# GEGLU of the second layer 5.7 batches behind its cross attention instead of 9, with x kept on chip between them

## The chip, the cores and the metric

The kernel runs on one core of one Trainium2 chip. The core has a TensorE (PE in the profile, with its weight loads listed apart as PEld), a VectorE (DVE), a ScalarE (ACT), a GpSimd (POOL), and a SyncE (SP), whose queue issues nearly all transfers of this kernel. The metric is device time in microseconds; lower is better. Each time is a median of several runs of the whole program. The profile is one separate execution of it.

## The reference

A tensor x of 32 batches of 112 rows and 256 columns goes through four layers that share one context of 32 times 375 rows and 256 columns. All is float32. Cut to what matters here:

```python
x = L0(x, ctx)        # grouped cross attention
# layer 1: three sublayers, each with a layernorm, a residual, and fake quantisation in the two attentions
x = attn(ln1(x), ln1(x), ...) + x                 # self attention       "l1s"
x = attn(ln2(x), context, ...) + x                # cross attention      "l1x"
hg = ln3(x) @ ff_w1 + ff_b1                       # GEGLU                "l1f"
a, g = split(hg, 2)
x = a * gelu(g, approximate=False) @ ff_w2 + ff_b2 + x
x = L2(x, ctx, ctx)   # cross attention "l2x" and feed-forward "l2f"
x = L3(ctx, x)        # causal self attention "l3s", cross attention "l3x", feed-forward "l3f"
```

`ff_w1` has 256 rows and 2048 columns, `ff_w2` 1024 rows and 256 columns. One batch does not depend on another, and a batch passes the sublayers in order.

## The kernel before

A **sweep** is one sublayer taken over all 32 batches. There are nine: `l0x, l1s, l1x, l1f, l2x, l2f, l3s, l3x, l3f`. A sweep is a list of **units** (one batch, or a pair of batches, `GB = 2`), and a unit is a list of **slots**: 8 per batch in `l1x` (two heads each), 4 per batch in `l1s` (four heads each), 8 per pair of batches in `l1f` (128 hidden columns each). A slot has stages (scores, softmax, transpose, product with V, closing step). `LAGS` says how many slots of its own sweep later each further stage is issued. Work that prepares a unit (loading x, layernorm statistics, applying the norm, projections) is a list of **atoms**, and `LEAD` says how many slots ahead of its place each atom is issued.

Sweeps run in pairs (`PAIRS`): `l0x` with `l1s`, `l1x` with `l1f`, `l2x` alone, `l2f` with `l3s`, `l3x` with `l3f`. `order` gives every slot a place on a planner's axis, in planner's units. A pair takes `dur` units per batch, the sum of its `SPAN` values (14 + 8 = 22 for `l1x` and `l1f`), and its second sweep starts `off` units after the first:

```python
off = max(GB * dur + self.DELAY[s] * dur, done + self.GAP - t0) if q else 0.0
```

`done` is where the pair ahead ends. For `l1f` the first term is 2 x 22 + 5 x 22 = 154. The pair ahead (`l0x` and `l1s`) ends 170 units after `l1x` has begun, so the second is 170 + 30 = 200, and `l1f` runs 200 units, or 9.1 batches, behind `l1x`. The ends overlap: `l1s` is still at work for the first 170 units of `l1x`, and `l1f` is alone for the last 200, since `l2x` begins where it ends (`OVER`).

**How x travels.** Within the pairs `l0x`/`l1s` and `l3x`/`l3f` the second sweep takes over the tile that the first one has written (`beside`). `l1x` and `l1f` are named in `AGAIN`: each loads x once for its norm and once more, late (the atom `again`), for its residual, and `l1x` stores its x to memory. All x tiles are of tag `x` with 11 buffers. During `l1x` the loads and stores of x are held back (`later`) and issued behind the next transposing transfer of `l1x` (`behind`), of which there are four per batch.

**Small tiles** have tags with buffers of their own: `ki` (6) for the quantised keys and the float tiles ahead of them, `ot` (7) for quantised queries, attention outputs and the split hidden tiles of `l2f` and `l3f`, `pp2` (4) for the softmax of four heads in `l1s` and `l3s` and for the masked queries of `l1x` (`queries_apart`).

The Python code issues instructions in the order of this plan. A scheduler that knows the buffers then settles each engine's instruction order and writes the semaphores. Each engine runs its list strictly in order. Lines that the text speaks of: L1126 scores of `l1x` (and of `l3x`), L1179 scores of `l1s` (and `l3s`), L1254 and L1294 the two products of `l1f`, L1283 its gate times value on VectorE, L458 the transposes of a normalised x, L456 the normalising itself, L441 the norm's statistics, L1227 the residual of `l1x`, L847 that of `l1f`, L386 the load of x, L411 its store, L900 the masked queries, L788 the scores of `l2x`.

Of the kernel before, what the change touches and what calls it, by code (L numbers as in the profile page):

```python
# [8 lines left out]
F32 = mybir.dt.float32  # L9
# [8 lines left out]
S = 112  # L18
# [42 lines left out]

class Kern:

    BUFS = dict(w=8, x=11, xh=4, ki=6, s1=9, sm=32, ot=7, pp2=4, k3=11, h=3, qs=2, k6=5)
    PBUFS = dict(sc=3, ps1=4, acc=1)

    LAGS = dict(
# [11 lines left out]
    LEAD = dict(  # L79
        l0x=dict(load=11, stats=10, apply=6, cload=11, cstats=8, cut=8, ctrans=5, q=4, k=[2, -2], v=-1),  # L80
        l1s=dict(load=5, stats=5, apply=3, q=2, k=2, v=1),
        l1x=dict(load=17, stats=12, apply=10, cload=14, cut=14, q=8, apart=[2, -1], k=4, v=-1, v2=[-2, -4, -6, -7], again=-7),
        l1f=dict(load=13, stats=11, apply=10, gate=2, gelu=1, again=-3),
        l2x=dict(load=10, stats=7, apply=6, cload=11, cut=7, q=4, k=[1, 1], v=0, vload=2),
        l2f=dict(load=6, stats=5, apply=3),
        l3s=dict(load=10, stats=8, apply=7, q=7, qload=3, k=6, v=3, c2=4, k2=1, v2=1),
# [285 lines left out]

    def beside(self, i):

        return any(self.sweeps[i : i + 2] == list(p) for p in PAIRS) and self.sweeps[i] not in self.AGAIN


    AGAIN = ("l1x", "l1f")

    def load_x(self, s, b):  # L380
        i = self.sweeps.index(s)
# [250 lines left out]
    def softmax4(self, sc, scale=None):  # L632

        nc = self.nc
        p = self.t([S, 4, S], F32, "pp2")
        sm = self.t([S, 4], F32, "sm")
        nm = self.t([S, 4], F32, "sm")
        nc.vector.tensor_reduce(nm, sc, AX.X, ALU.max, negate=True)
        if self.turn("exp4") == 1:
            nc.vector.tensor_tensor(p, sc, nm.unsqueeze(2).to_broadcast([S, 4, S]), ALU.add)  # L640
            nc.scalar.activation(p, p, AF.Exp, scale=1.0 if scale is None else scale)
            nc.vector.tensor_reduce(sm, p, AX.X, ALU.add)
            return p, sm
# [98 lines left out]
    def unit64(self, s, b0, i, qd, gb, W, g, cx, wd, wq, wk, wv, gqa, gkv, gvec, bvec):  # L742
# [33 lines left out]
        def mk(m):  # L776
# [22 lines left out]
            def c():  # L799
                if m == 0:  # L800
                    return
                vq = kv["v"]
                av = self.ps([128, 2, S])
                for mm in range(1 if gqa else 2):
                    for a in range(3):
                        ta = slice(a * S, (a + 1) * S)
                        for j in range(2):
                            hd = qd if gqa else 2 * mm + j
                            o = av[64 * j : 64 * j + 64]
                            nc.tensor.matmul(  # L810
                                o if gqa else o[:, mm, :],
                                vq[:, a, hd * 64 : hd * 64 + 64],
                                st["pt"][:, :, j, ta] if gqa else st["pt", mm][:, j, ta],
                                start=a == 0,
                                stop=a == 2,
                            )
                ot = st["ot"] = self.t([128, 2, 2, S], F32R, "ot")
# [25 lines left out]

    def residual(self, s, b0, g):

        for e, x in enumerate(g["xr" if s in self.AGAIN else "x"]):
            self.nc.vector.tensor_tensor(x, g["acc"][:, e, :], x, ALU.add)  # L847
            self.store_x(s, b0 + e, x)

# [46 lines left out]

    def queries_apart(self, i, c, bs):

        t = self.t([128, 8, S], BF16, "pp2")
        self.nc.gpsimd.tensor_tensor(  # L900
            t,
            i[:, c, bs].unsqueeze(1).to_broadcast([128, 8, S]),
            self.own.unsqueeze(2).to_broadcast([128, 8, S]),
            ALU.mult,
        )
        return t

    def fkq(self, ps, inv, shape):

        nc = self.nc  # L910
        p = shape[0]
        f = self.t(shape, F32, "ki")
        self.scale("fk", f, ps, inv[:p], MAGIC)
        self.eng("clip").tensor_scalar(f, f, MAGIC + 127.0, MAGIC - 128.0, ALU.min, ALU.max)
        return f

    def qk_atoms(self, lead, w, src, W, isq, quant, prm, put, tag=None, keep=None, apart=False):
# [4 lines left out]
        def half(c):  # L922
            if quant and c == 0:
                both = isq and not apart
                z["i"] = self.t([128, 2, 2, W] if both else [128, 2, W], BF16, "ot" if isq else "ki")
# [94 lines left out]
    def unit16(self, s, b0, i, gb, g, wd, quant, self_attn, qb, kb, vb, dl, gvec, bvec):  # L1020
# [54 lines left out]
        def av(heads, pt, first, octets, ahead=True):  # L1075
# [21 lines left out]
                        )  # L1097
            if octets:
                if octets[0] == 0:
                    st["ot"] = self.t([128, 2, 2, S], F32R, "ot")  # L1100
                oc = slice(octets[0], octets[-1] + 1)
                hi, lo = st["ot"][:, 0, oc, :], st["ot"][:, 1, oc, :]
                o = o[:, : len(octets), :]
# [60 lines left out]
        def quad(qd):  # L1164
# [28 lines left out]
            def b():  # L1193
                if quant:
                    z["pt"] = pt = self.t([128, 4, S], BF16, "s1")
                    nc.sync.dma_start_transpose(pt, z["pq"].rearrange("p h t -> p (h t)"))
                    return
                pst = self.ps([128, 4, S])
                for j in range(4):
                    nc.tensor.transpose(pst[:S, j, :], z["p"][:, j, :], self.ident[:S, :S])  # L1200
                z["pt"] = self.t([S, 4, S], F32, "pp2")
                self.copy("copy", z["pt"], pst[:S])

            def c():
# [13 lines left out]
        u.slots = [quad(qd) for qd in range(4)] if self_attn else [pair(pr) for pr in range(8)]  # L1218

        def fin():  # L1220
            x = st["xr"] if s in self.AGAIN else g["x"][i]
            po = self.ps([S, D])
            wo = wd["o"]
            self.bias_mm(s, po)
# [3 lines left out]
            self.store_x(s, b0 + i, x)  # L1228

        u.slots[-1].st[4] = fin  # L1230
        if s in self.AGAIN:
            u.atoms.append((L["again"], 0, lambda: st.update(xr=self.load_x(s, b0 + i))))
        return u


# [3 lines left out]
    def unitff(self, s, b0, gb, wd, gvec, bvec, b1, glu):  # L1239
# [33 lines left out]
        def mk(c):  # L1273
            z = {}

            def a():
# [10 lines left out]
                ul = z["ul"] = self.t([128, 2, W], F32R, "ot")  # L1287
                self.split(uu, ul[:, 0, :], ul[:, 1, :], ("upper", "lower"))

            def b():  # L1290
# [15 lines left out]
            return Slot(a, None, b)  # L1306

        u.slots = [mk(c) for c in range(8)]
        if s in self.AGAIN:
            u.atoms.append((L["again"], 0, lambda: g.update(xr=[self.load_x(s, b0 + i) for i in range(gb)])))  # L1310
        return u


# [40 lines left out]
    def order(self, units):  # L1354
# [5 lines left out]
        for p in [p for p in pairs if p]:  # L1360
# [4 lines left out]
            last = len(p)  # L1365
            for q, s in enumerate(p):
                n = sum(len(u.slots) for u in units[s])
                off = max(GB * dur + self.DELAY[s] * dur, done + self.GAP - t0) if q else 0.0
                k = 0
                for ui, u in enumerate(units[s]):  # L1370
                    for sl in u.slots:
# [4 lines left out]
        ev.sort(key=lambda e: e[:4])  # L1376
        return [(e[4], e[2], e[5]) for e in ev]

    DELAY = dict(l1s=3, l1f=5, l3s=3, l3f=2)
    GAP = 30.0  # L1380
    PAUSE = 4
    OVER = dict(l2x=0.0, l3x=34.0)

    def run(self):
# [231 lines left out]
```

## Time and profile before

| | |
|---|---|
| median of 3 runs | 4890.22 us (4889.1 to 4894.96) |
| profiled execution: time, span | 4897.09 us, 4895.3 us |
| TensorE busy, weight loads | 4482.3 us (92%), 3983.4 us (81%) |
| VectorE, ScalarE, GpSimd busy | 74%, 70%, 43% |
| mean granted TensorE clock | 0.963 |
| DMA | 674.54 MB, mean 138 GB/s |

The profile's page gives the busy share of each engine, a row of 40 slices of the span, and the chain of work that ended last. Several sweeps follow each other, so the share over the whole span is a mean over stages. A view by windows gives the same for chosen stretches of time, together with the clock that TensorE was granted. The view of one source line shows when its instructions ran, and so where a sweep begins and ends: the first score of `l1x` is at 1150 us, the last score of `l1s` at 1428 us, the first product of `l1f` at 1459 us, the last score of `l1x` at 2249 us, the first score of `l2x` at 2349 us.

### The profile page before, as it was taken

What the parts mean: (1) busy time and instruction counts of PE and PEld (TensorE: products, weight loads), DVE (VectorE), ACT (ScalarE), POOL (GpSimd) and SP (SyncE); (2) the same over time, 40 slices, a digit from 0 to 9 for tenths busy, and PEclk for the clock granted to TensorE, in tenths of its full rate; (3) what the DMA queues carried; (4) which work ended last, traced back from release to release, by engine and by line L of the source; (5) the groups of instructions that cost most, each with busy time, mean ns of one, the idle gap of its engine ahead of it and who ended that gap; (6) DMA issues with size and microseconds to landing.
All of it is one profiled execution on the core that took longest, in us unless ns stands there. A gap on an engine that the chain in (4) does not pass through costs nothing.

```text
span 4895.3 us, 111536 instructions
## 1 busy us (share of the span) xinstructions
PE 4482.3 (92%) x37824; PEld 3983.4 (81%) x37824; DVE 3618.5 (74%) x9806; ACT 3406.4 (70%) x10644; POOL 2119.8 (43%) x3674
## 2 busy tenths in 40 slices
PE   6999999998778999999999999998999886898999
PEld 5888888886667888888999999997888885787878
DVE  4788888888888888885788888886555554777776
ACT  4788888887767777774677777774555444677776
POOL 4455555555443333432333333334333332566665
PEclk9999999999889999999999999999999997999999
DMA  4433333334666565664455555543666667666663
GB/s 103 126 85 86 82 85 86 84 78 123 139 132 137 140 150 146 151 161 119 129 142 144 142 144 143 143 130 112 197 188 184 200 182 205 169 168 163 162 162 85
DMA packets 585415, 674.54 MB, mean 138 GB/s; under 512 B 318688, under 2 KB 495056, under 8 KB 584656
## 3 DMA queue, kind: packets, MB, share of 16 engines
q1 hardware_dynamic: 584848, 667.40, 52.2%
q8 instruction: 305, 5.00, 0.5%
q14 instruction: 262, 2.15, 0.1%
HBM read 323.55 MB, written 173.02 MB: 101 GB/s over the span
## 4 chain that ended last, share of the span: by engine, by line
PE 39%; DMA 7%; DVE 5%; ACT 1%; issue 1%; SPq 1%; POOL 1%; ACTq 0%; DVEq 0%; POOLq 0%
PE ps L679 6%; PE ps L235 5%; PE ps L236 4%; PE ps L237 4%; PE sc L788 3%; PE ps L810 3%; PE ps L1090 3%; DMA qs<-dq_l3s 2%; PE sc L1126 2%; DMA k<-cd 2%; PE acc L235 1%; PE acc L237 1%; PE acc L236 1%; PE ps L1254 1%; DVE sm L621 1%
## 5 line engine op out<-in xcount | busy, mean ns | idle before, releaser
L217 POOL TENSOR_SCALAR k<-k,sm 112x375 f32<-112x375 f32 (+1 forms) x1536 | 936.7, 622 | 1036.0 <-DVE sm L661 459.6
L200 ACT ACTIVATE k<-ps 125x336 f32<-125x336 f32 (+4 forms) x2005 | 914.0, 469 | 425.4 <-PE ps L237 185.9
L621 DVE TENSOR_REDUCE sm<-sc 112x1 f32<-112x375 f32 x1792 | 944.8, 539 | 150.0 <-PE sc L788 89.7
L627 ACT ACTIVATE k<-sc,sm 112x375 f32<-112x375 f32 x1536 | 881.2, 579 | 104.1 <-DVE sm L621 84.7
L679 PE MATMUL ps<-ident,k 112*125 112x112 f32 x4608 | 733.2, 277 | 15.2 <-issue 4.0
L679 PEld LDWEIGHTS ps<-ident,k 112*125 112x125 f32 x4608 | 649.2, 190 | 71.7 <-issue 43.7
L788 PE MATMUL sc<-k,qs 128*112 128x376 f32 x2048 | 539.9, 356 | 19.9 <-ACT k L627 9.7
L235 PE MATMUL ps<-w,k 128*125 128x256 f32 (+2 forms) x1344 | 431.4, 321 | 30.6 <-ACT k L627 15.5
L235 PE MATMUL ps<-h,w 128*128 128x224 f32 x1408 | 410.9, 299 | 43.4 <-DVE h L202 17.1
L710 DVE TENSOR_TENSOR k<-ps,k 64x376 fp32r<-64x376 f32 x640 | 350.2, 547 | 123.3 <-ACT k L200 108.0
L202 DVE COPY k<-ps 125x336 f32<-125x336 f32 (+2 forms) x619 | 289.3, 468 | 170.3 <-PE ps L237 69.5
L236 PE MATMUL ps<-h,w 128*128 128x224 f32 x1408 | 393.7, 282 | 0.8 <-DVE h L231 0.5
L237 PE MATMUL ps<-h,w 128*128 128x224 f32 x1408 | 392.8, 282 | 0.0
L236 PE MATMUL ps<-w,k 128*125 128x256 f32 (+2 forms) x1344 | 390.6, 291 | 0.0
L237 PE MATMUL ps<-w,k 128*125 128x256 f32 (+2 forms) x1344 | 389.4, 290 | 0.0
L235 PE MATMUL ps<-k,w 128*128 128x376 f32 x896 | 341.3, 381 | 41.4 <-DMA k<-cd 26.1
L810 PE MATMUL ps<-k,k 125*64 125x112 f32 (+1 forms) x4608 | 350.0, 296 | 3.6 <-DVE k L202 1.5
L213 POOL TENSOR_SCALAR k<-k,sm 112x375 f32<-112x375 f32 x256 | 165.5, 647 | 416.5 <-DVE sm L661 326.6
L788 PEld LDWEIGHTS sc<-k,qs 128*112 128x112 f32 x2048 | 304.1, 177 | 49.3 <-ACT k L627 24.4
L235 PEld LDWEIGHTS ps<-w,k 128*125 128x125 f32 (+2 forms) x1344 | 264.0, 196 | 79.0 <-ACT k L627 26.7
L235 PEld LDWEIGHTS ps<-h,w 128*128 128x128 f32 x1408 | 273.2, 197 | 67.3 <-issue 29.7
L627 ACT ACTIVATION_READ_ACCUMULATOR k<-sc,sm 112x1 f32 x1536 | 324.0, 211 | 0.0
(213 smaller groups left out, 12592.3 us busy)
## 6 DMA issues: line engine op xcount, KB each, us to landing
qs<-h SPq DMA_DIRECT2D x512, 224.0 KB
k<-k SPq DMA_DIRECT2D x192, 376.0 KB
k<-cd SPq DMA_DIRECT2D x64, 752.0 KB
vd<-k SPq DMA_DIRECT2D x128, 375.0 KB
k<-vd SPq DMA_DIRECT2D x128, 375.0 KB
qs<-dq_l3s SPq DMA_DIRECT2D x256, 112.0 KB
qs<-dq_l3x SPq DMA_DIRECT2D x256, 112.0 KB
x<-xd SPq DMA_DIRECT2D x224, 112.0 KB
```

The costliest lines, as they stand in the source:

```text
L200: self.nc.scalar.activation(out, in_, AF.Identity)
L202: self.nc.vector.tensor_copy(out, in_)
L217: self.nc.gpsimd.tensor_scalar(out, in_, by, 1.0, ALU.mult, ALU.mult)
L235: mm(out, lhs(0), rhs(0), start=start, stop=False)
L236: mm(out, lhs(0), rhs(1), start=False, stop=False)
L237: mm(out, lhs(1), rhs(0), start=False, stop=stop)
L621: nc.vector.tensor_reduce(nms[j], sc[j][:, :n], AX.X, ALU.max, negate=True)
L627: nc.scalar.activation(p[:, j, :n], sc[j][:, :n], AF.Exp, bias=nms[j], scale=1.0 if scale is None else scale, accum_out=sm[:, j : j + 1])
L679: self.nc.tensor.transpose(pst[:TB, a * S : (a + 1) * S], p[:, j, a * TB : (a + 1) * TB], self.ident[:S, :S])
L710: nc.vector.tensor_tensor(ks[o, j, :], pk[r, :TE], ks[r, j, :].bitcast(F32), ALU.subtract)
L788: nc.tensor.matmul(sc[:, :TE], qs[:, hd, q, bs], kk, start=q == 0, stop=q == 1)
L810: nc.tensor.matmul(o if gqa else o[:, mm, :], vq[:, a, hd * 64 : hd * 64 + 64], st["pt"][:, :, j, ta] if gqa else st["pt", mm][:, j, ta], ...
```

## The change

`AGAIN` is taken out. `l1x` and `l1f` are now a pair like the others: `l1x` loads x once, adds its residual into the same tile, `l1f` takes its norm from that tile and adds its own residual into it, and stores it. That takes out 32 stores and 96 loads of x (112 x 256 float32 each). The tag `x` has 13 buffers instead of 11.

`DELAY` of `l1f` goes from 5 to 3 and `GAP` becomes a value per sweep, -44 for `l1f` (30 for `l3s` and `l3f` as before, 0 for `l1s`, for which the first term decides as before). `off` of `l1f` is then max(44 + 66, 170 - 44) = 126 units, or 5.7 batches. `l1f` starts 44 units before the end of `l1s`.

`ki`, `ot` and `pp2` become one tag, `m`, with 15 buffers (17 in the three before). The leads follow: `l1x` loads x 14 slots ahead instead of 17, `l1f` takes x, its statistics and its norm 10 slots ahead (13, 11 and 10 before). Past the last slot of `l1x`, its outstanding stages are issued at half the distance.

```diff
-    BUFS = dict(w=8, x=11, xh=4, ki=6, s1=9, sm=32, ot=7, pp2=4, k3=11, h=3, qs=2, k6=5)
+    BUFS = dict(w=8, x=13, xh=4, m=15, s1=9, sm=32, k3=11, h=3, qs=2, k6=5)
...
-        l1x=dict(load=17, stats=12, apply=10, cload=14, cut=14, q=8, apart=[2, -1], k=4, v=-1, v2=[-2, -4, -6, -7], again=-7),
-        l1f=dict(load=13, stats=11, apply=10, gate=2, gelu=1, again=-3),
+        l1x=dict(load=14, stats=12, apply=10, cload=14, cut=14, q=8, apart=[2, -1], k=4, v=-1, v2=[-2, -4, -6, -7]),
+        l1f=dict(load=10, stats=10, apply=10, gate=2, gelu=1),
...
     def beside(self, i):
 
-        return any(self.sweeps[i : i + 2] == list(p) for p in PAIRS) and self.sweeps[i] not in self.AGAIN
-
-
-    AGAIN = ("l1x", "l1f")
+        return any(self.sweeps[i : i + 2] == list(p) for p in PAIRS)
...
-        p = self.t([S, 4, S], F32, "pp2")
+        p = self.t([S, 4, S], F32, "m")
...
-        for e, x in enumerate(g["xr" if s in self.AGAIN else "x"]):
+        for e, x in enumerate(g["x"]):
...
-        f = self.t(shape, F32, "ki")
+        f = self.t(shape, F32, "m")
...
-                    st["ot"] = self.t([128, 2, 2, S], F32R, "ot")
+                    st["ot"] = self.t([128, 2, 2, S], F32R, "m")
...
-            x = st["xr"] if s in self.AGAIN else g["x"][i]
+            x = g["x"][i]
...
-        if s in self.AGAIN:
-            u.atoms.append((L["again"], 0, lambda: st.update(xr=self.load_x(s, b0 + i))))
...
-                off = max(GB * dur + self.DELAY[s] * dur, done + self.GAP - t0) if q else 0.0
+                off = max(GB * dur + self.DELAY[s] * dur, done + self.GAP[s] - t0) if q else 0.0
...
-    DELAY = dict(l1s=3, l1f=5, l3s=3, l3f=2)
-    GAP = 30.0
+    DELAY = dict(l1s=3, l1f=3, l3s=3, l3f=2)
+    GAP = dict(l1f=-44.0, l3s=30.0, l3f=30.0, l1s=0.0)
...
-                    j = mine[s][m] if m < len(mine[s]) else mine[s][-1] + m - len(mine[s]) + 1
+
+                    o = m - len(mine[s]) + 1
+                    j = mine[s][m] if o <= 0 else mine[s][-1] + ((o + 1) // 2 if s == "l1x" else o)
```

More of the change, by code (lines that the diff above doesn't have):

```diff
@@ L816, in c @@
                             )
-                ot = st["ot"] = self.t([128, 2, 2, S], F32R, "ot")
+                ot = st["ot"] = self.t([128, 2, 2, S], F32R, "m")
                 self.copy("ohi", ot[:, 0], av)
@@ L897, in queries_apart @@
     def queries_apart(self, i, c, bs):
-        t = self.t([128, 8, S], BF16, "pp2")
+        t = self.t([128, 8, S], BF16, "m")
         self.nc.gpsimd.tensor_tensor(
@@ L924, in half @@
                 both = isq and not apart
-                z["i"] = self.t([128, 2, 2, W] if both else [128, 2, W], BF16, "ot" if isq else "ki")
+                z["i"] = self.t([128, 2, 2, W] if both else [128, 2, W], BF16, "m")
             pq = self.ps([128, W])
@@ L1200, in b @@
                     nc.tensor.transpose(pst[:S, j, :], z["p"][:, j, :], self.ident[:S, :S])
-                z["pt"] = self.t([S, 4, S], F32, "pp2")
+                z["pt"] = self.t([S, 4, S], F32, "m")
                 self.copy("copy", z["pt"], pst[:S])
@@ L1286, in a @@
                 self.shift("relu", uu, pf, b1[:, c : c + 1], AF.Relu)
-                ul = z["ul"] = self.t([128, 2, W], F32R, "ot")
+                ul = z["ul"] = self.t([128, 2, W], F32R, "m")
                 self.split(uu, ul[:, 0, :], ul[:, 1, :], ("upper", "lower"))
@@ L1308, in unitff @@
         u.slots = [mk(c) for c in range(8)]
-        if s in self.AGAIN:
-            u.atoms.append((L["again"], 0, lambda: g.update(xr=[self.load_x(s, b0 + i) for i in range(gb)])))
         return u
```

## The prediction

> **What bounds the kernel now.** I read the busy shares first, then cut the layer-1 part into stretches, since the change acts there alone. The stretches follow the source-line views: scores of `l1x` run from 1150 to 2249 us, `l1s` ends at 1428, `l1f` starts at 1459, `l2x` at 2349.
>
> ```profile
> 1150.00:1340.00 190.00, 145.58 (x1084) 121.24 (x1083) 164.75 (x450) 136.25 (x420) 87.47 (x160) 0.86 0.63 138
> 1340.00:1455.00 115.00, 85.47 (x640) 69.29 (x640) 93.61 (x259) 78.01 (x238) 47.85 (x87) 0.83 0.65 134
> 1455.00:1600.00 145.00, 131.03 (x978) 113.55 (x979) 117.23 (x323) 108.01 (x296) 58.06 (x89) 0.92 0.60 134
> 1600.00:2249.00 649.00, 602.04 (x4563) 527.95 (x4562) 538.09 (x1493) 494.54 (x1343) 241.49 (x380) 0.97 0.63 149
> 2249.00:2350.00 101.00, 94.68 (x531) 85.62 (x530) 45.59 (x121) 28.13 (x55) 20.75 (x34) 0.97 0.42 111
> ```
>
> The columns are the stretch, its length, busy time of PE, PEld, DVE, ACT, POOL, then granted clock, DMA share and GB/s. While `l1s` and `l1x` overlap (the first two lines), PE is busy 77% and 74% at a clock of 0.86 and 0.83: full-clock work is 0.66 and 0.62 of the time. With `l1x` and `l1f` together (fourth line) it is 602 x 0.97 / 649 = 0.90. In the last line `l1f` is nearly alone: PE 94% busy, DVE 45%, ACT 28%. So work of `l1f` waits for a tail that PE alone bounds, while two hundred microseconds earlier PE has a third of its time free. What holds the first stretches is a chain through several engines, not one full engine (DVE is at 87%, then 81%):
>
> ```profile
> POOL k L213 <- DVE sm L661: 21.6, 15, 2.3
> PEld ps L235 <- ACT k L627: 14.8, 6, 6.3
> POOL pp L213 <- DVE sm L661: 12.0, 7, 3.3
> ACT sm L624 <- DVE sm L621: 11.3, 9, 2.3
> ```
>
> (Waits in 1340 to 1455 us: total, times, longest.) No pair holds more than a fifth of the 115 us.
>
> **What l1f costs.** Its two products in the tail (2275 to 2345 us), the group view:
>
> ```profile
> L1254 PE MATMUL ps<-h,w 128*128 128x224 f32 x199 | 42.7, 353 | 0.0
> L1294 PE MATMUL acc<-w,s 128*112 128x256 f32 x121 | 31.4, 379 | 0.0
> ```
>
> Busy time per record is 42.7/199 = 0.215 and 31.4/121 = 0.26 us. The page holds 1024 and 512 such records, 32 and 16 per batch: 6.9 + 4.2 = 11.0 us of PE per batch. On DVE, 4 x 0.45 (L1283) plus statistics, norm and residual at 0.4 each and some small ones: 3.5 us per batch.
>
> **The change, part by part.** How far the order moves I take from the instruction order of the two built programs, which holds no times. Before, the first L1254 stands behind 130 of the 512 `l1x` scores; after, behind 80. 80 scores fall in the first line above (41 and 39 records), so the new start is at 1340 us. When `l1x` issues its last score, 128 of 512 L1254 products are still to come before, about 72 after: 56/16 = 3.5 batches of `l1f` leave the tail.
>
> 1. Tail: 3.5 x 11.0 = -38.5 us.
> 2. Where they go: `l1s` ends in the new order at `l1x` score 117, so 37 scores (2.3 batches) now run as three sweeps, with 43 L1254 products, 2.7 batches of `l1f`. The second line above holds 48 scores, 3 batches: 38.3 us each, PE 85.5 x 0.83 / 3 = 23.7 at full clock, DVE 31.2. PE then needs 2.3 x 23.7 + 2.7 x 11.0 = 84 us, at the 0.90 of the joint stretch 94. DVE needs 2.3 x 31.2 + 2.7 x 3.5 = 81, at the 87% of the first line 93. So 94 where 2.3 x 38.3 = 88 were: +6. Bounds: 0 if it all fits into PE's gaps; +36 if nothing does and the clock stays (2.7 x 11.0 / 0.83). I take +6, the nearest rows being the 0.90 and the 87% that this stage reaches.
> 3. The joint stretch then has no slow start. Before, scores 117 to 512 took 0.7 batch x 38.3 + 794 = 821 us (1455 to 2249); after, 24.7 batches at the rate of the fourth line (632 of 1024 L1254 records in 649 us, so 19.75 batches, 32.9 each) = 813: -8. Bounds: -3 at the mean of the old joint part (794/24 = 33.1); -20 if the gaps of 7% shrink a little, to 32.4.
> 4. The tail's reload goes. Once per run PE waits for x that went to memory and back:
>
> ```profile
> 2254.25 0.60 SPq L411
> 2254.90 0.42 SPq L386
> 2255.36 0.44 SPq L386
> 2255.85 3.69 DMA x<-xd
> 2259.56 0.44 DVE sm L441
> ```
>
> (Chain of the end, by time.) The wait at L458 there is 5.5 us. In its place comes the direct chain of the last pair: residual 0.42, two statistics 0.8, norm 0.4, the power on POOL 0.84 and hand-overs, some 3 us, with only 7 PE instructions between. Net -2.5; bounds -5.5 and 0.
> 5. A new wait for every pair: `l1f`'s norm now hangs on `l1x`'s residual just written. PE's list has 125 instructions between the last product of the residual and the transposes (L458); a pair of batches has 544 and takes 2 x 32.9 us, so that is 15 us; DVE has 41 to do meanwhile. The nearest row is `l3x` to `l3f`, already on chip, with 167 to 182 instructions between. Its L458, 4250 to 4800 us:
>
> ```profile
> its engine sat idle before it (us, times) until:
>   POOL xh L456: 5.5, 19
>   DVE xh L456: 1.1, 5
> ```
>
> 6.6 us over the pairs: I take +6, bounds 0 and 82 (15 pairs at the 5.5 us of point 4, all uncovered). Behind L458 on PE stand `l1x`'s own scores, so such a stall holds both sweeps.
> 6. SP issues 128 transfers fewer, 112 KB each, 14.7 of 674.5 MB, and the stores and loads queued behind `l1x`'s transposing transfers shrink. A loss is excluded, and a DMA share of 0.6 bounds nothing in these stretches: 0. At best the waits on transfers between 1340 and 1455 us go (4.5 for the context, 4.3 for x, 3.4 for a transpose): -12.
> 7. The load of x comes 14 slots ahead: one transposing transfer of `l1x` lies between load and statistics instead of two, 8 us. `l1f`'s loads stood that close before; the statistics' waits for x were 17.1 us, 6 times, over the run. 0, at worst 15 x 2.9 = 43 on DVE, of which the 10-slot norm covers the most.
> 8. Two more units of GELU run among softmaxes: four table loads at 1.28 us, 5 us on ScalarE, at 68% in its stretch. 0, at worst 5.
> 9. One tag of 15 for 17: in the new program's order at most 13 are alive. Before, `pp2` had all 4 alive and `ki` all 6 in the stretch of `l1s` with `l1x`. So no new wait, maybe fewer: 0, at best 5 batches x (38 - 33) = -25 in the first line. In layer 3, where `pp2` was full too, the order shifts by tens of instructions within a unit. Between 3400 and 4050 us PE waits longest for queries from memory (31.7 us, 10 times), which no tag changes: 0, and within 10 either way, a third of that wait.
>
> Sum: -38.5 + 6 - 8 - 2.5 + 6 = -37 us. The profiled execution (4897.1, span 4895.3) would become 4860; it lies 7 over the median, so against 4890.2 the forecast is **4853 us**.
>
> [...] The granted clock was 0.83 with PE gaps and 0.97 without, as shown. [...]
>
> **Rivals.** *The overlap does not absorb* (17%): the three-sweep stretch is held by the softmax chain, and `l1f`'s instructions lengthen it in full. Point 2 becomes +36: 4883. For it: DVE 87%, POOL waiting for L661. Against: PE idle and throttled there, and DVE idle for 21 of the 115 us, where `l1f` asks it for 9.5.
> *The chain of point 5 is late* (12%, the slower side): PE stands before L458 in each of some 15 pairs. At 5.5 us each, 82 instead of 6: 4929. It decides from (37 + 6) / 15 = 2.9 us a pair. For it: 125 instructions where `l3x` has 170, and DVE 83% busy here. Against: the 0.3 us of the `l3f` row.
> *The shared tag frees the start* (9%): -25 more, 4828.
>
> **How the numbers follow.** The forecast has 62% (4833 to 4868: points 2, 3 and 5 at their nearer bounds). What a measurement here can tell from no change is about 0.2%, 9.8 us. The first rival falls half within that, half faster (9% and 8%). Faster: 62 + 9 + 9 = 80%; same 8%; slower 12%. The range leaves out the late chain and the far end of the last rival: 4822 to 4889.
>
> **What would show it.** First L1254 near 1340 us; the clock in the next 90 us above 0.9 with PE near 90%; 4.5 batches of `l1f` after the last `l1x` score, and some 63 us from there to the first L788 instead of 101; first L788 near 2312 instead of 2349; the rest as long as before. Wrong if L458 shows waits on DVE of over 2 us a pair between 1400 and 2250, if `l1x` needs more than 45 us a batch while three sweeps run, or if layers 2 and 3 change by over 10 us.

## The result, and the profile after

The changed kernel takes 5027.8 us (median of 5 runs, 5021.3 to 5034.1) where the kernel before took 4890.2: ratio 1.0274, 95% interval 1.0255 to 1.0292. The forecast was 4853. The profiled execution has a span of 5024.7 us (before 4895.3) and a mean granted clock of 0.957 (before 0.963).

In the changed kernel the lines are numbered 3 to 5 lower: scores of `l1x` L1123 (before L1126), products of `l1f` L1249 and L1289 (L1254, L1294), gate times value L1278 (L1283), GELU L1266, transposes of a normalised x L455 (L458), the norm L453, statistics L438, the power that ends them L413, residuals L1224 and L844. Kernels made from the one before keep its numbers.

The view by source line cuts the span at the same events as before (us):

| stretch | before | after | difference |
|---|---|---|---|
| start to the first score of `l1x` | 1150 | 1189 | +39 |
| first to last score of `l1x` | 1099 | 1285 | +186 |
| last score of `l1x` to the first of `l2x` (the tail) | 100 | 73 | -27 |
| scores of `l2x` | 992 | 987 | -5 |
| last score of `l2x` to the first of `l3x` (mostly `l3s`) | 770 | 718 | -52 |
| from there to the end | 784 | 772 | -12 |

The tail shrank, `l3s` gained, and both are swamped by the scores of `l1x`. How sharp such a table is: three profiled executions whose code in layer 1 is the same (before and two experiments below, `pt_ot` and `l3_ot`) have 1199, 1206 and 1210 us for layer 1 (second and third row together). Differences below about 11 us are not read.

The windows of the changed kernel that answer to those of before: `l1s` with `l1x` up to the first product of `l1f`; the three sweeps together; the joint stretch of `l1x` and `l1f`, in two; the tail. Columns as there: stretch, length, busy PE, PEld, DVE, ACT, POOL, granted clock, DMA share, GB/s.

```profile
1189.00:1395.00 206.00, 151.99 (x1108) 128.04 (x1107) 170.94 (x474) 141.15 (x431) 93.91 (x169) 0.83 0.58 126
1395.00:1490.00 95.00, 78.12 (x605) 64.88 (x602) 77.42 (x203) 70.87 (x206) 34.62 (x65) 0.96 0.54 110
1490.00:1800.00 310.00, 249.02 (x1801) 218.18 (x1798) 230.51 (x601) 194.91 (x525) 97.85 (x157) 0.91 0.49 111
1800.00:2474.00 674.00, 551.74 (x3942) 483.46 (x3941) 501.03 (x1283) 429.82 (x1157) 204.03 (x334) 0.89 0.48 112
2474.00:2548.00 74.00, 63.67 (x363) 56.83 (x361) 34.61 (x89) 21.50 (x44) 16.72 (x28) 0.93 0.48 108
```

The three sweeps (second line) take the time forecast, 95 us at a clock of 0.96, though PE is busy 82% in them and not near 90%. Of the 186 us that the scores of `l1x` lost, 16 lie in the first line (206 us for 190), 7 in the second (95 for the 88 of the prediction's point 2) and 163 in the joint stretch (984 for the 821 of its point 3). In the fourth line, the larger part of the joint stretch, PE is busy 82% at 0.89, so full-clock work fills 551.74 x 0.89 / 674 = 0.73 of the time, where before it was 0.90. No other engine took its place: DVE fell from 83% to 74%, ACT from 76% to 64%, GpSimd from 37% to 30%. All engines wait more. From 1490 to 2474 us a batch takes 984 / 24.7 = 39.8 us instead of 32.9.

Who waits, in the larger part of the joint stretch: the three longest totals of PE, then the wait of DVE that bears on the first of them (waits: us in total, times, longest):

```profile
PE ps L235 <- DVE s L1278: 30.9, 7, 5.2
PE ps L235 <- ACT m L211: 27.4, 9, 3.8
PE ps L455 <- DVE xh L453: 22.8, 9, 2.7
```

```profile
DVE sm L438 <- DMA x<-xd: 23.8, 7, 4.2
```

A pair of batches takes 80 us, so 674 us are 8.4 pairs and each of the three PE lines is one stand per pair. Together 81.1 / 8.4 = 9.6 us per pair. The pair got 2 x (39.8 - 32.9) = 13.9 longer; the rest is, by an estimate, about what the clock makes (0.89 for 0.97 is 8%, and 8% of 66 us is 5). PE's busy time per pair grew by about as much, from 61.0 to 64.9 us (602.04 us for 632 products L1254, 551.74 us for 544 products L1249, 64 to a pair).

One such pair, by time (timeline: start, duration, engine, line; in brackets the idle time before it and what ended it; lines between are left out):

```profile
2032.27 0.43 DVE L438 BATCH_NORM_STATS2 sm<-x 112x6 f32<-112x256 f32 x1 [3.52 <-DMA x<-xd]
...
2035.36 0.44 DVE L1278 SCALAR_TENSOR_TENSOR s<-ps,vec_L_xattn_ff_b,qs 128x224 f32<-128x224 f32 x1
...
2035.86 0.58 PE L235 MATMUL ps<-w,k 128*125 128x256 f32 x1 [4.49 <-DVE s L1278]
```

```profile
2053.59 1.28 ACT L1266 ACT_TABLE_LOAD   x1
2054.88 1.70 ACT L1266 ACTIVATE qs<-qs 128x1792 f32<-128x1792 f32 x1
2056.48 1.70 ACT L211 ACTIVATE m<-ps,magic,iv 128x256 f32<-128x256 f32 x4
...
2057.54 0.58 PE L235 MATMUL ps<-w,k 128*125 128x256 f32 x1 [3.78 <-ACT m L211]
...
2058.94 0.40 DVE L438 BATCH_NORM_STATS2 sm<-x 112x6 f32<-112x256 f32 x1
...
2061.48 1.77 POOL L231 TENSOR_TENSOR k<-k,k 128x752 fp32r<-128x752 f32 x1 [1.71 <-issue]
...
2063.21 0.70 POOL L413 TENSOR_TENSOR sm<-sm,nhalf 112x2 f32<-112x2 f32 x1
...
2063.94 0.73 DVE L453 TENSOR_SCALAR xh<-x,sm,sm 112x256 f32<-112x256 f32 x2 [2.08 <-POOL sm L413]
...
2064.50 0.60 PE L455 MATMUL ps<-ident,xh 112*128 112x112 f32 x2 [2.66 <-DVE xh L453]
```

Stand one: DVE waits 3.5 us for the x that `l1x` loads, now 14 slots ahead, and the instructions queued behind that wait on DVE, L1278 among them, hold PE for 4.5 us. Stand two: GELU with its table load holds ScalarE for 3 us, `l1x`'s quantising (L211) stands behind it, PE waits 3.8. Stand three: `l1f`'s statistics start at 2058.94, the power (L413) stands on GpSimd behind a splitting of 1.77 us, the norm follows at 2063.94, and PE has been waiting for it for 2.7 us.

Stand three sits where point 5 of the prediction looked, but not for its reason. Followed batch by batch, the later of the two residuals of `l1x` that this norm hangs on (L1224) ran at 2045.21, and its statistics at 2059.98: x lay ready for over 14 us. Over the pairs from 1500 to 2474 us it is 13.1 us at least.

### The profile page after: what moved, and what is told of

Same layout as the page of the kernel before. It is cut to its first block, busy times and chain, and to the rows that moved or that the text cites. A ratio compares the mean times of both kernels' runs of the same rounds, so it can differ in the third digit from the quotient of the medians.

```text
span 5024.7 us, 111377 instructions
## 1 busy us (share of the span) xinstructions
PE 4511.3 (90%) x37824; PEld 3998.1 (80%) x37824; DVE 3686.0 (73%) x9805; ACT 3419.1 (68%) x10649; POOL 2087.4 (42%) x3674
## 5 line engine op out<-in xcount | busy, mean ns | idle before, releaser
L217 POOL TENSOR_SCALAR k<-k,sm 112x375 f32<-112x375 f32 (+1 forms) x1536 | 921.1, 612 | 1039.5 <-DVE sm L658 419.2
L624 ACT ACTIVATE k<-sc,sm 112x375 f32<-112x375 f32 x1536 | 882.3, 579 | 114.1 <-DVE sm L618 85.3
L235 PE MATMUL ps<-w,k 128*125 128x256 f32 (+2 forms) x1344 | 446.3, 332 | 132.6 <-DVE s L1278 48.5
L235 PE MATMUL ps<-h,w 128*128 128x224 f32 x1408 | 406.1, 295 | 37.7 <-DVE h L202 11.6
L235 PEld LDWEIGHTS ps<-w,k 128*125 128x125 f32 (+2 forms) x1344 | 275.6, 205 | 175.0 <-DVE s L1278 52.6
L236 PE MATMUL ps<-w,k 128*125 128x256 f32 (+2 forms) x1344 | 401.5, 299 | 0.0
L237 PE MATMUL ps<-w,k 128*125 128x256 f32 (+2 forms) x1344 | 400.0, 298 | 0.0
L236 PE MATMUL ps<-h,w 128*128 128x224 f32 x1408 | 390.4, 280 | 1.4 <-POOL h L231 1.1
L237 PE MATMUL ps<-h,w 128*128 128x224 f32 x1408 | 388.1, 278 | 0.0
L235 PE MATMUL ps<-k,w 128*128 128x376 f32 x896 | 336.8, 376 | 35.0 <-DMA k<-cd 22.4
L624 ACT ACTIVATION_READ_ACCUMULATOR k<-sc,sm 112x1 f32 x1536 | 324.4, 211 | 0.0
L235 PEld LDWEIGHTS ps<-h,w 128*128 128x128 f32 x1408 | 269.5, 195 | 62.9 <-issue 13.4
```

Of the source, the lines that this page charges most:

```text
L217: self.nc.gpsimd.tensor_scalar(out, in_, by, 1.0, ALU.mult, ALU.mult)
L235: mm(out, lhs(0), rhs(0), start=start, stop=False)
L236: mm(out, lhs(0), rhs(1), start=False, stop=False)
L237: mm(out, lhs(1), rhs(0), start=False, stop=stop)
L624: nc.scalar.activation(p[:, j, :n], sc[j][:, :n], AF.Exp, bias=nms[j], scale=1.0 if scale is None else scale, accum_out=sm[:, j : j + 1])
```

## The experiments

Where the text says layer 1 it means first score of `l1x` to first score of `l2x`.

| run | ratio to before (95% interval) | start | layer 1: scores + tail | `l2x` end to `l3x` |
|---|---|---|---|---|
| before | 1 | 1150 | 1099 + 100 | 770 |
| after | 1.0274 (1.0255, 1.0292) | 1189 | 1285 + 73 | 718 |
| tag_only | 1.0052 (1.0038, 1.0065) | 1187 | 1140 + 102 | 727 |
| tag_x13 | 1.0039 (1.0020, 1.0057) | 1188 | 1137 + 102 | 732 |
| load17 | 1.0181 (1.0155, 1.0206) | 1188 | 1221 + 72 | 728 |
| far | 1.0129 (1.0102, 1.0157) | 1189 | 1186 + 101 | 725 |
| far17 | 1.0090 (1.0065, 1.0114) | 1192 | 1171 + 100 | 718 |
| off170 | 1.0137 (1.0115, 1.0160) | 1187 | 1206 + 90 | 721 |
| far17s | 1.0018 (1.0003, 1.0033) | 1192 | 1123 + 101 | 731 |
| off170s | 1.0025 (1.0009, 1.0041) | 1188 | 1138 + 91 | 723 |
| after_st11 | 1.0061 (1.0038, 1.0085) | 1192 | 1183 + 70 | 726 |
| after17s | 0.9996 (0.9978, 1.0015) | 1186 | 1152 + 70 | 727 |
| after_ki | 1.0179 (1.0156, 1.0201) | 1166 | 1250 + 71 | 721 |
| kisep | 0.9974 (0.9962, 0.9986) | 1170 | 1121 + 101 | 723 |
| pp6 | 1.0057 (1.0039, 1.0076) | 1152 | 1133 + 102 | 777 |
| pt_ot | 1.0009 (0.9996, 1.0022) | 1151 | 1105 + 101 | 778 |
| p_ot | 1.0037 (1.0018, 1.0055) | 1175 | 1104 + 100 | 762 |
| l3_ot | 0.9898 (0.9880, 0.9915) | 1155 | 1107 + 103 | 722 |
| after17s_ki | 0.9963 (0.9947, 0.9979) | 1170 | 1149 + 72 | 723 |
| best | 0.9875 (0.9856, 0.9895) | 1151 | 1130 + 72 | 723 |

### The one tag alone

The kernel before with every tile of `ki`, `ot` and `pp2` in one tag `m`, in `tag_only` with 11 tiles of x, in `tag_x13` with 13; nothing else. The line of `tag_x13`:

```diff
-    BUFS = dict(w=8, x=11, xh=4, ki=6, s1=9, sm=32, ot=7, pp2=4, k3=11, h=3, qs=2, k6=5)
+    BUFS = dict(w=8, x=13, xh=4, m=15, s1=9, sm=32, k3=11, h=3, qs=2, k6=5)
```

> The kernel before, with one edit: ki, ot and pp2 become the tag m with 15 buffers; x keeps 11 tiles, the reload and the 200 units stay. The changed kernel's trace shows three differences: l1x begins 39 us later (1189 against 1150), layer 1 takes 159 us longer from there to l2x (1358 against 1199), and from the end of l2x on it is some 65 us shorter. If the tag makes the first and the last of these, this run takes 4890 + 39 - 65 = 4864, with l1x beginning near 1189. If 13 x tiles make them, it takes 4890 within 10. If the tag is also what slows layer 1, it takes about 5020.

> As tag_only, and x has 13 tiles. Everything but the schedule of layer 1 and the x kept on chip is now as in the changed kernel. If these two make the whole loss in layer 1, this run is 159 us under the changed kernel: 4869, with l1x beginning at 1189 and 1199 us from there to l2x. If buffers make the loss in layer 1, it stays near 5028.

Measured: start +37, scores of `l1x` about +40, `l3s` -40: within what such a table can tell, the tag makes the whole loss of the start and the whole gain of `l3s`, and it is 0.4 to 0.5% slower. But it makes only 40 of the 186 us that the scores of `l1x` lost. The number of x tiles changes nothing that these runs can tell.

### The distance or the leads

`load17` is the changed kernel with one lead put back. `far` is the changed kernel at the old distance, 200 units; `far17` is both; `off170` lies between the two, at 170 units, which stands at the same phase of the pair of batches as 126 (44 units are one pair). All kernels made from the changed one keep its other edits, among them the one that issues the last stages of `l1x` at half the distance.

```diff
# load17
-        l1x=dict(load=14, stats=12, apply=10, cload=14, cut=14, q=8, apart=[2, -1], k=4, v=-1, v2=[-2, -4, -6, -7]),
+        l1x=dict(load=17, stats=12, apply=10, cload=14, cut=14, q=8, apart=[2, -1], k=4, v=-1, v2=[-2, -4, -6, -7]),
# far: x=16, m=13, l1x load 14; far17: the same with load=17
-    DELAY = dict(l1s=3, l1f=3, l3s=3, l3f=2)
-    GAP = dict(l1f=-44.0, l3s=30.0, l3f=30.0, l1s=0.0)
+    DELAY = dict(l1s=3, l1f=5, l3s=3, l3f=2)
+    GAP = dict(l1f=30.0, l3s=30.0, l3f=30.0, l1s=0.0)
# off170: x=15, m=13, l1x load=17
+    GAP = dict(l1f=0.0, l3s=30.0, l3f=30.0, l1s=0.0)
```

> The changed kernel with one edit: l1x loads x 17 slots ahead, as before, not 14. VectorE stood 3.5 us in each pair of batches before the statistics of x, for the load (23.8 us, 7 times, in the joint stretch), and TensorE 4.5 us after it. If the late load is the cause of that gap, the waits of L438 for x go and the joint stretch loses 4.5 us or more in each of some 14 pairs: 4965 or less. If the loads only show the queue's delay, or if the chain from l1x's residual to l1f's norm decides, within 15 us of 5028.

> The changed kernel with l1f back at 200 units, 9.1 batches behind l1x, x still kept on chip: x gets 16 tiles and m 13 for it. Leads stay as in the changed kernel, so x is loaded 14 slots ahead. If the short way from l1x's residual to l1f's norm is the cause in layer 1, that way is now 3 batches longer, the gaps at L455 and behind it go, and layer 1 takes near 1199 us: 4870. If the late load is the cause, it still has it: 4960 or more. If buffers are the cause, about 5028.

> The changed kernel with l1f back at 200 units and x loaded 17 slots ahead: x on chip, 16 x tiles, 13 of m. Each of the two edits alone took away 46 and 72 us. With both, what is left over tag_x13 (4914, where x is reloaded and layer 1 takes 1240 us from the first l1x score to the first l2x score) is the worth of x on chip itself. If late load and short way are the whole loss, layer 1 takes 1240 or a little less and the run 4905 to 4915. If 13 m tiles or x on chip cost something of their own, above 4930.

> The changed kernel with x loaded 17 slots ahead (as load17, 4982) and l1f 170 units behind l1x, not 126: one pair of batches (44 units) more, so that l1f meets l1x in the same phase of its pair, and only the way from residual to norm is longer. x has 15 tiles, m 13. In load17 TensorE stood twice in each pair: about 2.5 us at L455 for the norm and 3.8 us behind ScalarE (L211). If the short way makes both, both go and layer 1 falls from 1293 to about 1240: 4925. If the second is the phase (GELU with its table loads standing ahead of l1x's quantising on ScalarE), it stays and layer 1 takes about 1270. If the distance does not matter, 4982.

Putting `l1x`'s load back gains 65 us of layer 1 in the trace, and 46 us of the whole time by the ratios: stand one is real and has a price of that size. The rest is not the distance: with the load at 17, 170 units (1296) and 126 units (1293) take the same, and even 200 units (`far17`) stay at 1272, 32 over the one tag alone. `far`, with the load at 14, has 1287 (its profiled execution lies 21 us over its median). The PE waits of `off170`, 1800 to 2300 us, still show stands two and three:

```profile
PE ps L235 <- ACT m L211: 26.5, 7, 3.8
PE ps L455 <- DVE xh L453: 16.1, 6, 2.9
```

So the prediction's slower rival, a chain through the residual that a shorter distance makes late, falls for the changed kernel: 44 more units of slack moved layer 1 by 3 us, and x lay ready for 13 us. (The whole time of `off170` is 0.4% shorter than that of `load17`; the intervals just overlap, and the tiles differ too.) At 200 units PE hardly waits for the norm (`far17`, 1800 to 2350 us: 2.0 us, once). Its stand there is another one, the scores L1123 waiting for exponentials on ScalarE (L624): 40.9 us in 8 times. A thing all these kernels share is `l1f`'s own leads, 10, 10, 10.

### One slot between `l1f`'s statistics and its norm

First with the longer distances, then at the changed distance itself. `l1f`'s load lead moves no transfer any more, x being on chip; what counts is that the statistics are issued one slot ahead of the norm again.

```diff
# far17s from far17, off170s from off170
-        l1f=dict(load=10, stats=10, apply=10, gate=2, gelu=1),
+        l1f=dict(load=13, stats=11, apply=10, gate=2, gelu=1),
# after_st11 from the changed kernel; after17s: also l1x load=17
-        l1f=dict(load=10, stats=10, apply=10, gate=2, gelu=1),
+        l1f=dict(load=11, stats=11, apply=10, gate=2, gelu=1),
```

> far17 (old distance and phase, x on chip, one tag, l1x load 17) with l1f's own leads put back: load 13, stats 11, apply 10 for 10, 10, 10. Its layer 1 was 1272 us where the one tag with x reloaded took 1240. If l1f's shorter leads make the 32 us, layer 1 falls to about 1240 and the time to about 4910. If x staying on chip itself makes them (its norm now hangs on the residual), layer 1 stays within 10 of 1272 and the time at 4941.

> off170 (GEGLU 170 units behind, so the new phase within the pair, load 17) with l1f's leads 13, 11, 10. Theory: two of the stands per pair of batches have separate causes, the leads and the phase. The wait at L455 for the norm (18.7 us, 7 times, in 1800 to 2350) should go, as statistics and apply are a slot apart again; the wait of PE at L235 for ACT L211 behind GELU (26.5 us, 7 times) should stay, as it comes from the phase. Layer 1 then 1296 - 25 = about 1270, time 4940. Rival, the distance or the leads make both: both waits go, 1245, time 4915. Rival, neither is the leads: 1296, 4965.

> The changed kernel with one slot between l1f's statistics and its norm (load 11, stats 11, apply 10 for 10, 10, 10), l1x's load still 14. With 170 and 200 units of distance l1f's own leads were worth 67 and 48 us of layer 1. Theory: the missing slot makes them at 126 units too; layer 1 from 1358 to about 1300, the wait at L455 for the norm gone, time 4970. Rival, the chain through the residual is late at 126 units: a statistic asked for a slot earlier then waits for the residual, layer 1 stays within 10 of 1358 or grows, time 5028 or more.

> The changed kernel with both leads: l1x's load 17 for 14 and l1f's load 11, stats 11, apply 10. Alone the first was worth 65 us of layer 1, the second some 55. If they are two separate stands in a pair of batches they add: layer 1 about 1235, time 4920. If one stand hides behind the other they add to less: 1270, 4955.

All four gained, and more than expected. With the load of `l1x` at 17 the slot is worth 48 us of layer 1 at 200 units, 67 at 170 and 72 at 126 (`load17` to `after17s`); with the load at 14 it is worth 105 (the change to `after_st11`). At 200 units it was the wait of the scores for the exponentials that fell, from 40.9 to 2.3 us (`far17s`, 1800 to 2300 us). `off170s` was meant to keep stand two, since I took GELU's place for a matter of phase. It did not: both lines went from L235 and L455, and a smaller wait came in the place of the second. The PE waits of `off170s`, same window:

```profile
PE ps L1123 <- ACT m L211: 17.6, 7, 2.5
```

At the changed distance, `after_st11`, 1800 to 2375 us: stand three is gone, stand two has left L235 for L1123 and is shorter, stand one is left as it was.

```profile
PE ps L235 <- DVE s L1278: 26.1, 7, 4.4
PE ps L1123 <- ACT m L211: 18.9, 8, 2.5
```

With the load of `l1x` back as well, `after17s`, that goes too. Its windows for the three sweeps and the joint stretch, and one pair from its timeline:

```profile
1385.00:1481.00 96.00, 79.91 (x604) 65.51 (x601) 80.79 (x214) 74.58 (x211) 35.62 (x68) 0.95 0.48 105
1481.00:1800.00 319.00, 286.98 (x2157) 251.92 (x2156) 268.82 (x710) 229.28 (x623) 115.72 (x187) 0.96 0.58 127
1800.00:2338.00 538.00, 480.19 (x3586) 422.14 (x3585) 446.42 (x1168) 391.38 (x1055) 187.75 (x301) 0.95 0.61 129
```

```profile
2036.01 0.39 DVE L438 BATCH_NORM_STATS2 sm<-x 112x6 f32<-112x256 f32 x1
...
2037.73 1.70 ACT L1266 ACTIVATE qs<-qs 128x1792 f32<-128x1792 f32 x1
...
2038.42 0.92 DVE L453 TENSOR_SCALAR xh<-x,sm,sm 112x256 f32<-112x256 f32 x2
...
2042.64 1.01 PE L455 MATMUL ps<-ident,xh 112*128 112x112 f32 x4 [1.75 <-ACT k L624]
```

The norm is done at 2039.3. PE comes to its transposes 1.5 us later and then waits 1.75 us for ScalarE, not for the norm. GELU stands ahead of `l1x`'s quantising here as well: L211 starts at 2039.5. But PE has products to run until 2038.9, and waits 1.65 us where it waited 3.78.

The slot also uses up most of the slack behind the residual. The later residual of this pair ran from 2030.82 to 2031.24 us (L1224), and its statistics start at 2036.01, 4.8 us after it; in the changed kernel it was 14.4. A slot is nearly 9 us here (a pair of 69 us has 8), so at 126 units a second slot would ask for the statistics before their data is there. No run tried it.

The clock is back at 0.95, and a batch takes 857 / 24.7 = 34.7 us. Alone, the slot takes 102 us from the scores of `l1x` (1285 to 1183) and the load 64 (to 1221); together 133 (to 1152). They overlap: some of each stand was covered by another.

### What of the one tag costs, and what gains

```diff
# kisep, from before: ki stays apart (6 tiles), ot and pp2 are one tag of 11
+    BUFS = dict(w=8, x=11, xh=4, ki=6, s1=9, sm=32, m=11, k3=11, h=3, qs=2, k6=5)
# after_ki, from the changed kernel: ki apart (6 tiles), m=10
# pp6, from before: ot=5, pp2=6
# pt_ot, from before (L1201, the transposed probabilities of l3s)
-                z["pt"] = self.t([S, 4, S], F32, "pp2")
+                z["pt"] = self.t([S, 4, S], F32, "ot")
# p_ot, from before (L635): the probabilities of l1s alone
-        p = self.t([S, 4, S], F32, "pp2")
+        p = self.t([S, 4, S], F32, "ot" if scale is not None else "pp2")
# l3_ot, from before: the probabilities of l3s alone (L635), and L1201 as in pt_ot
+        p = self.t([S, 4, S], F32, "ot" if scale is None else "pp2")
```

> The kernel before with ki kept apart (6) and only ot and pp2 merged, as m of 11; everything else as before. With all three merged (tag_only, 4924) l1x began 37 us later and layer 3's first part took 43 us less. In tag_only GpSimd waited 97 us (53 before) at the clipping of a ki tile for ScalarE, ahead of l0x's softmax. If ki's six buffers hold the quantising of l1s back to where it is needed, and giving it fifteen lets the scheduler put it early, l1x begins near 1150 here, and layer 3 keeps its 43 us: 4850. If ot or pp2 does it, l1x begins near 1187: 4900 to 4925.

> The kernel before with three tags as they were, ot 5 instead of 7 and pp2 6 instead of 4 (no more than 5 of ot were alive, and all 4 of pp2). If four pp2 tiles are what slowed the softmax of l3s, layer 3's first part takes 43 us less and nothing else changes: 4850. If the gain there comes from ot, it stays at 4890 or, should 5 be too few, above.

> The kernel before with one word changed: l3s's transposed probabilities (L1201) from tag ot (7 tiles) instead of pp2 (4). Layers 0 to 2 keep their tags. If the 4 tiles of pp2 and what pairs with them held l3s (POOL pp for DVE sm, 134 us), l3s falls from 770 towards 725 and the time to about 4850, under both kernels. pp2 with 6 tiles did not do that (777), so the rival: it is the order that follows from one tag for l3s's quantising and softmax tiles alike, or ki's, and l3s stays near 770, time 4890.

> The changed kernel with the tag ki apart again (6 tiles, the other two tags one of 10). On the kernel before, that took half of the one tag's loss in the start (20 of 37 us) and half of layer 1's (19 of 43), and kept l3s's gain. If the tag adds up with the rest, the changed kernel gains 30 to 40 us: 4990. If the stands in layer 1 hide it, only the start moves: 5008. Same as the changed kernel, 5028, if the tag's effect there has another source.

> The kernel before with l3s's probabilities alone (L635, the quantised sweep) taken from tag ot instead of pp2; layers 0 to 2 keep their tags. (The run pt_ot moved a tile that l1s alone uses, so it says nothing of l3s.) If what gains in l3s is that these two tiles share one tag, l3s goes from 770 to about 725 and the time to 4850. If it is the larger number of tiles (11 for 7 and 4), 7 are too few and l3s stays near 770 or grows: 4890 to 4930.

> The kernel before with l3s's two tiles moved from pp2 to ot, its probabilities (L635 where nothing is quantised: l3s, not l1s) and their transposes (L1201), so that l3s has ot and pp2 as one tag in effect, of 7 tiles, and layers 0 to 2 keep theirs. To set right what the expectation of p_ot says: the quantised sweep is l1s, L1201 is l3s's; p_ot therefore tried l1s, pt_ot half of l3s. If sharing gains in l3s: 770 to about 725, time 4850. If the number of tiles does: l3s with 7 for 11 stays near 770 or grows, 4895 to 4930.

The expectation of `p_ot` is wrong in two places: it takes the quantised sweep for `l3s`, and the tile of `pt_ot` for one of `l1s`. It is the other way round, as that of `l3_ot` says. `p_ot` is read so here.

*Start.* `p_ot` moves one tile of `l1s` into the tag of its queries, and the start goes from 1150 to 1175 us. `kisep`, which shares the same two, loses 20; all three tags together lose 37. So about half of the loss or more comes from `l1s`'s probabilities sharing buffers with its queries, the rest from `ki` joining. *Scores of `l1x`.* `p_ot` leaves them alone (1104), `kisep` has +22, the full tag +40: half is `ki`. In the changed kernel `ki` apart (`after_ki`) is worth 23 us in the start and 36 in layer 1. With the leads put back (`after17s_ki` against `after17s`) it is worth 16 in the start and nothing in layer 1 (1221 and 1221), so in layer 1 the tag's price does not simply add to that of the leads.

*`l3s`.* Two more tiles for `pp2` (`pp6`) gave nothing, `l3s`'s transposes alone in the other tag (`pt_ot`) nothing. `l3_ot` adds the probabilities: 722, as good as one tag of 11 or 15, with only the 7 tiles of `ot`. So it is sharing that gains, not the number of tiles. Whether the probabilities alone would do was not tried. The GpSimd waits in 3450 to 4050 us, before and then `l3_ot`:

```profile
POOL pp L1187 <- DVE sm L661: 134.3, 54, 6.8
POOL ot L231 <- DVE ot L202: 94.4, 40, 6.4
```

```profile
POOL ot L231 <- DVE ot L202: 145.2, 51, 6.2
...
POOL ot L1187 <- DVE sm L661: 43.0, 59, 2.0
```

Before, GpSimd stood 2.5 us each time at the product with the reciprocal (L1187), with other work queued behind it; after, 0.7 us, and the waiting is at the splits (L231). The order of its list has changed, which is what the scheduler makes of the tags. Why it settles on this order was not tried.

### A version that beats both

```diff
# after17s_ki: after17s with ki apart (ki=6, m=10)
# best: after17s with the tags of before, ot one smaller, and l3s's two tiles in ot as in l3_ot
+    BUFS = dict(w=8, x=13, xh=4, ki=6, s1=9, sm=32, ot=6, pp2=4, k3=11, h=3, qs=2, k6=5)
```

> As after17s, with ki a tag of its own (6 tiles, the other two as one of 10). On the changed kernel that took 23 us from the start and 36 from layer 1, there with the stands of the leads still in it. With start 1167 and layer 1 1215 the time is about 4880, 0.3% under the kernel before; with nothing from layer 1, 4900.

> after17s (the change with l1x's load 17 and l1f's statistics a slot before its norm) with the tags of before, ot one tile smaller (6) to make room for x, and l3s's two tiles in ot as in l3_ot. The start should be that of before, 1150 for 1186; layer 1 1221 or, without the one tag's share, 1190; if l3s keeps the one tag's 725: 4850 or below, under both kernels. Against it: six tiles of ot may be too few for the queries of l1x (pp6, with five, lost 36 us in layer 1).

`after17s_ki` takes 4883.0 us, 0.9963 of before; `best` 4838.2, 0.9875. `best` is the fastest, but most of that is `l3s`: `l3_ot`, with layer 1 untouched, has 0.9898, and the two intervals overlap. What the shorter distance itself gives is then small. Its windows for the joint stretch:

```profile
1441.00:1800.00 359.00, 320.97 (x2455) 284.95 (x2455) 292.88 (x811) 263.32 (x712) 138.69 (x215) 0.96 0.59 126
1800.00:2281.00 481.00, 435.01 (x3290) 388.62 (x3289) 385.22 (x1071) 357.51 (x969) 172.31 (x274) 0.95 0.61 134
```

The tail is 31 us shorter than in `l3_ot`, and the scores of `l1x` take 23 longer. The same comparison under one tag, with good leads in both, is `far17s` (200 units) against `after17s` (126): tail -31, scores +29.

## Why the prediction was wrong

A ladder of the parts, by the ratios: the one tag +0.4% (`tag_x13`); x kept on chip at the old distance -0.2% (`far17s`, which also has the last stages of `l1x` at half the distance and other numbers of tiles); the shorter distance -0.2% (`after17s`); the shorter leads +2.8% (the change). In us of some 4897: +19, -10, -11, +136. The neighbouring intervals of the first rungs touch, so their sizes are good to about 10 us; the last is far outside. Each of the steps:

1. *Tail, -38.5:* 148 of the 1024 products L1249 start after the last score of `l1x`, 4.6 batches for the 4.5 forecast. But the tail is 73 us, not 63. Most of the 10 us is one wait of PE for the last transposing transfer of `l1x`. The distance does not make it: `far17s`, at the old distance, has it too. PE's wait in the tail, the changed kernel and then `far17s`:

```profile
PE ps L1087 <- DMA k<-k: 8.1, 1, 8.1
```

```profile
PE ps L1087 <- DMA k<-k: 6.3, 1, 6.3
```

Kernels made from the one before have 1.1 us (`l3_ot`) or none (`tag_x13`) there. What bears on it is the edit that issues the last stages of `l1x` at half the distance. It has no term in the sum, and it was not run alone, so this cause is not shown.

2. *Three sweeps, +6:* right in its size; 95, 96 and 95 us in the change, `after17s` and `best`, for 94. The stretch before it, which the sum left at 190 us, took 206, 199 and 195.
3. *Joint stretch, -8:* wrong by itself, before any lead is counted. 813 us were forecast; with good leads it took 857 (one tag) or 840 (`best`), 34.7 and 34.0 us a batch for 32.9. This is where the tail's gain went. In `best` PE's longest waits there are for the norm (L455, 23.6 us, 7 times) and for exponentials on ScalarE (L235 for L624, 19.4 us, 18 times); in `l3_ot`, at the old distance, none is over 11.8. The wait for the norm goes with the tags as well as with the distance: at 126 units and with the same leads `after17s_ki`, with `ki` apart, has 39.4 us of it (9 times, 1465 to 2319 us), and `after17s`, with one tag, none. In `best` it ends a chain that does begin at the residual: L1224 at 1976.66, the statistics at 1979.03 and 1981.04, the power at 1985.94, the norm at 1988.21, after which PE has waited 3.8 us. So there point 5's chain has little to spare. Whether more distance would cure it with these tags was not tried.
4. *Reload in the tail, -2.5:* the 5.5 us wait is gone, 1.9 us at L455 is left. Right.
5. *New wait at L458, +6 with bounds 0 and 82:* **the step that failed most.** It took the residual as the start of the chain and PE's 125 instructions after it as the cover. In the changed kernel the residual is over 13 us early. The chain starts where the statistics are issued, and the diff put those into the same slot as the norm (11 and 10 became 10 and 10). That edit stands in the diff and has no term in the sum. Its price is 105 us of layer 1 as it stood, beyond the bound of 82, and 72 with the load already back: with the slot back, stand two shrank and stand three went, and the clock in the long joint stretch came from 0.89 to 0.95. The signal named for being wrong (over 2 us a pair at L458) did show: 22.8 us in 8.4 pairs, 2.7 each.
6. *128 fewer transfers, 0:* 674.5 MB became 659.8. x on chip as a whole is worth some -10 us (`far17s` against `tag_x13`), which is no more than these runs can tell; the part of the transfers in that was not separated.
7. *Load 14 slots ahead, 0, at worst 43 on DVE:* the wait was as bounded (23.8 us, 3.4 each), but it was priced on the engine that waits. PE stands longer (4.4 each) for what is queued behind it. 65 us of layer 1 alone, 32 with the slot already back.
8. *Table loads, 0, at worst 5:* priced on ScalarE, where their number was not the point. GELU with its load stands ahead of `l1x`'s quantising with or without the slot; in the pairs shown, what PE still has to run meanwhile makes the difference. With the slot back 18.9 of 27.4 us remain, at another line.
9. *One tag, 0 and `l3s` within 10:* wrong both ways, +37 in the start, +40 in the scores of `l1x`, -40 in `l3s`. Fewer tiles alive than buffers was taken to mean that no order changes. The sign named for being wrong, layer 3 off by over 10 us, did show.

The forecast's narrower band, 4833 to 4868, does not follow from the bounds it names: points 2, 3 and 5 at their nearer bounds give 4841 to 4858.

Of the rivals, "the overlap does not absorb" fell in its own stretch (95 us); its loss came later, in the joint one. "The chain of point 5 is late" had the side and the place, but not the mechanism: 44 units more did not cure it. Its side came true by luck, not by its reasoning. "The shared tag frees the start" had the wrong sign.

## What to carry to other kernels

Price every number of a lead table, the small ones first: two steps of one chain issued in the same slot can leave PE's in-order list too little to run between them, even where their data lay ready 13 us before. Moving the first step ahead spends that slack (14.4 us became 4.8 in the pairs shown). Price a wait for a transfer at the engine that waits for what is queued behind it, not at the engine that stands (here 4.4 us each on PE for 3.4 on DVE). And merging buffer tags is a change of instruction order, good in one stage and bad in another: try it per stage (here one sweep's two tiles gained 1%, the same idea in another sweep put its end 25 us later).

## What the runs showed of the hardware

The granted clock of the joint stretch went with a few stands of PE. Three per pair of batches (longest 5.2, 3.8 and 2.7 us; the changed kernel, 1800 to 2474 us) went with 0.89, two (longest 3.8 and 2.9, `off170`, 1800 to 2300 us) with 0.93, one of up to 4.4 us and smaller ones with 0.95 (`after_st11`, 1800 to 2375 us). Without the large ones it was 0.95 (`after17s`, 1800 to 2338 us) and 0.97 (before, 1600 to 2249 us). In the changed kernel some 4 of the 14 us that a pair got longer lie outside the three stands; that the clock makes them is the estimate made with the waits above. What makes the clock fall no run here shows.
